# Third layer of a four-layer cross-attention stack: TensorE keeps the written order, dense work spread evenly over the attention units

## The chip, the cores and the metric

One core of a Trainium2 chip runs the whole program in one launch. TensorE (PE) multiplies, VectorE (DVE), ScalarE (ACT) and GpSimd (POOL) do the rest, and every transfer is issued from SyncE's queue (SP). The metric is device time in microseconds; before the change the median of three runs is 1750.37 us (1742.13 to 1756.63).

## The reference, cut to what matters

Four cross-attention layers act one after the other on `x` (8 batches, 256 tokens, 512 features); each takes its keys and values from the same context `ctx` (8, 256, 512).

```python
x = L0(x, ctx)   # layer norm, 16 heads, output projection, then a feed-forward block of width 2048
x = L1(x, ctx)   # one head of width 512:
#   scores = (x Wq^T)(ctx Wk^T)^T / sqrt(512);  x + alpha * softmax(scores) (ctx Wv^T) Wo^T
x = L2(x, ctx)   # 32 query heads of width 16 on 8 key/value heads:
#   q = x Wq + bq;  k = ctx Wk + bk;  v = ctx Wv + bv
#   scores = q k^T / 4 + mask[l, s];  out = softmax(scores) v Wo + bo
#   layer norm of (out + x), times gamma, plus beta
x = L3(x, ctx)   # 16 heads on the layer norm of ctx; x + tanh(gate) * out Wo^T
```

All of it is fp32. The change is about L2, the third layer, and about L1, whose work is done in its shadow.

## The kernel before, in words

**Number format.** Most products use a split of each fp32 operand into a high and a low part (`split`, L175) and three matmuls (`PASSES`: hi-hi, hi-lo, lo-hi). A projection (`feat_mm`, L208, output with features on partitions; `tok_mm`, L222, output with tokens on partitions) is therefore 12 matmuls for one output bank.

**Stages.** First L0's projections and attention, then its feed-forward block (`FeedForward`), whose last of 16 steps is mixed with the beginning of L1 (`mix(ff.steps(1), l12_fill())`). Then one loop, `pipeline` (L717), runs 64 attention *units*: 32 of class `Gqa` (L2: batch b, feature quarter ft) and 32 of class `Mha` (L3).

**A unit of L2.** It has four methods that run in different turns of the loop. In turn t, unit t does A, unit t-1 does B, unit t-2 does C and D.
- A(h), h = 0 to 3 (L1172): two score matmuls (L1179, 512 columns) into the two `sm` banks; DVE adds the mask and takes the maxima with four instructions (L1189). After h = 3, DVE writes the negated maxima as a high and low part.
- B (L1207): PE transposes these (L1210), ACT copies them, SP stores them into rows 96 to 99 of the unit's query stack.
- C(i), i = 0 to 3 (L1225): two matmuls give transposed scores less the maximum (L1233) in the two `st` banks. For the places listed in `POOL_ADDS`, ACT copies the bank out (L1243) and POOL adds the mask (L1244); for the others DVE adds it straight from the bank (L1246). ACT takes the exponential of both halves (L1248).
- The value run `AV(kt)` (L1254) multiplies the probabilities by the values: four matmuls of 32 output rows which use different quarters of the array, a denominator among their rows. AV(0) stands at the end of C(2), AV(1) at the beginning of D.
- D then copies the result out (L1272), stores it to DRAM and loads it in another layout (L1273, L1277); E, later, divides and splits it into `at` (L1285 to L1290).

The unit's query stack comes from `q2d` in DRAM (L1169), its keys from `k2d` (L1170); both loads are issued one turn ahead.

**Dense work.** Everything that isn't attention is written as Python generators kept by `Fillers`. Each `yield` gives a nominal cost in us. After each quarter of a turn the loop calls `fill.tick(us, budget/4)`, which runs generators until the budget of nominal us is spent; in L2 the budget is `B2` = 13 a turn. `fill.until(cond)` runs them regardless of the budget until something that must come first has been written: `before2` (L1442) demands that batch b's queries are written (`ready[0] > b`) one turn ahead of the batch's first unit. The generators of this part:
- `l12_fill` (L1298): for each batch b, L1 and L2's projections. `Context(b).load` fetches weights (`ws`, 1 MB each, three buffers) and the context (`nat`, two buffers, shared with the q stores), `scores_side` multiplies the context by folded weights, `kv` makes L2's keys and values (L1050 stores), `rows` L1's value rows; class `L1` does `features` (transposes), `scores` (softmax on the way), `transpose`, `output`; then `to_feat` and `feat_out` (L354) make L2's queries and store them to `q2d` (L374). Batch b's part starts `LEAD` = 4 turns ahead of its first unit.
- `l2_post` (L1391): the output projection with `wo` and `at`, residual, layer norm, store to `h2d`. It is put at the head of the queue when a batch's last E has been written. It frees the residual's buffer, which a later `L1.load` takes (`free_h`).
- `l3_fill` (L1346): L3's weights and projections; added in `before2` at the last batch of L2.

**What sets the order.** The Python order is only the order in which instructions are written. A list scheduler with a timeline model of the engines then fixes one static order for each engine: among the instructions that are ready in its model it takes the one of highest priority, by order of writing, with A and C raised by `tc.high_priority(PRIO)`. So TensorE may run later units' scores while written-earlier dense work waits. On the chip each engine runs its static order and waits on semaphores.

**Buffers.** PSUM has eight banks: three for dense work and transposes (`pp`), two `sm`, two `st`, one `av`. Probabilities use three `P` buffers and, for batches up to NB - 3, two halves of `pk`.

Of the kernel before, what the change touches and what calls it, by code (L numbers as in the profile page):

```python
# [23 lines left out]
B2, B3 = 13, 5.0  # L24
LEAD = 4
# [43 lines left out]
L3_SB = dict(L_SB, wk="a8-9", wv="a2,a7", x8="a4-5", st5="a3", vo="b3,b4", V="v0-1",  # L69
# [6 lines left out]
def tile_xattn_stack(  # L76
# [131 lines left out]
    def feat_mm(pt, ws, ft, xs, n=D):  # L208
        k = 0
        for kc in range(4):  # L210
            for wj, xj in PASSES:
                nc.tensor.matmul(  # L212
                    pt[:, :n],
                    lhsT=sel(ws, wj, kc)[:, ft * P : (ft + 1) * P],
                    rhs=sel(xs, xj, kc),
                    start=(k == 0),
                    stop=(k == 11),
                )
                k += 1
        return 12 * n * MMUS  # L220

    def tok_mm(pt, xs, tt, ws, n=D):  # L222
        k = 0
        for kc in range(4):
            for xj, wj in PASSES:
# [7 lines left out]
                k += 1  # L233
        return 12 * n * MMUS

# [19 lines left out]

    class Fillers:


        def __init__(self):
            self.q = []  # L260
            self.now = 0.0
            self.acc = 0.0
            self.step = 0

# [14 lines left out]
        def one(self):  # L279
            for e in self.q:  # L280
# [5 lines left out]
        def adv(self, e):  # L286
            try:
# [3 lines left out]
                return  # L291
            if c < 0.0:
# [5 lines left out]
        def until(self, cond):  # L298
            n = 0
            while not cond():  # L300
                self.adv(self.q[0])
                n += 1
                assert n < 9000

# [49 lines left out]
    def feat_out(ph, b, xs, wq, qd, biases):  # L354
        g, bb = divmod(b, 2)
        for f2 in range(2):
            pt = ph.PS("pp")
            for i in range(2):
                c = feat_mm(pt[:, i * 256 : (i + 1) * 256], wq, 2 * f2 + i, xs, n=256)
# [18 lines left out]
            yield 2 * c  # L378
# [338 lines left out]
    def pipeline(units, before, after, budget):  # L717
        n, lag = len(units), 2
        late = []
        for t in range(n + lag + 1):  # L720
            fill.step = t
            if t == 0:
# [9 lines left out]
            for i in range(nch):  # L732
# [6 lines left out]
                if i == nch // 2 - 1 and w:  # L739
                    w.B()  # L740
                fill.tick(us, budget(t) / nch)
                while late and late[0][0] <= fill.now:
# [3 lines left out]
            if v:  # L746
                v.D()
                late.append((fill.now + v.ELAG, t - lag))
# [259 lines left out]
    class Context:  # L1008
# [19 lines left out]
        def scores_side(self):  # L1028
            self.es = kept("ec")[:, 0:1024].rearrange("p (k t) -> p k t", k=4)
            for i in range(2):  # L1030
                pt = ph5.PS("pp")
                for k in range(2):
                    c = feat_mm(pt[:, k * 256 : (k + 1) * 256], self.we, 2 * i + k, self.xs, n=256)
                p3 = pt.rearrange("p (k t) -> p k t", k=2)
                nc.scalar.copy(self.es[:, 2 * i : 2 * i + 2], p3)
                yield 2 * c
            self.wn = load_hl(ph5, mnd, "ws")
# [32 lines left out]
        def rows(self, kt):  # L1070
            self.cp = kept("ec")[:, 1024:].rearrange("p (k n) -> p k n", k=2)
            pt = ph5.PS("pp")
            c = tok_mm(pt, self.xs, kt, self.wn)
            nc.scalar.copy(self.cp[:, kt, :], pt)
            yield c

    class L1:
# [17 lines left out]
        def scores(self, es):  # L1095
            sc = 1.0 / 512.0**0.5
            pt = ph5.PS("pp")
            for qt in range(2):
                for kc in range(4):
# [6 lines left out]
                    )  # L1106
            nb = ph5.T([P, 2], F, "sm1")
# [16 lines left out]
            yield 16 * D * MMUS  # L1124
# [29 lines left out]
    POOL_ADDS = ((0, 1), (1, 1), (2, 1))  # L1154

    class Gqa:
# [59 lines left out]
        def probs(self):  # L1216
            last["p"] = (last.get("p", -1) + 1) % 5
            if self.b < NB - 2 and last["p"] % 2:
# [5 lines left out]
        def C(self, i):  # L1224
            ph = self.ph  # L1225
            kt, hp = divmod(i, 2)
            if i == 0:
                self.av = ph.PS("av")
# [21 lines left out]
            if i == 2:  # L1250
                self.AV(0)


        def AV(self, kt):  # L1254
            with Burst() as mm:
                for hp in (1, 0):
                    for u in range(2):
                        g = 2 * u + hp
                        mm(
                            self.av[32 * g : 32 * g + 32, :],  # L1260
                            self.vo[:, kt, 2 * self.ft + u, :],
                            self.ps[2 * kt + hp][:, u].rearrange("p h t -> p (h t)"),
                            kt == 0,
                            kt == 1,
                        )

        def D(self):
            self.AV(1)
# [28 lines left out]

    def l12_fill():  # L1298
# [4 lines left out]
        yield from c.scores_side()  # L1303
        yield from c.kv()
        for kt in range(2):
            yield from c.rows(kt)
        a.features()
        for b in range(NB):
# [5 lines left out]
            if d:  # L1314
                d.load()
                yield from d.scores_side()
            a.transpose()
            if d:
                nxt = L1(b + 1)
                nxt.load()  # L1320
                while fill.step < 4 * b - 2 and b > 1:
                    yield -1.0
                yield from d.kv()
            yield from a.output(c.cp)
            if b == 0:
                while ff.fc < 4 * NG:
                    yield -0.5
                wts["q2"] = load_w(ph5, w2q, "wq", scale=0.25, stag="nat")
                rows["bo"], rows["g"], rows["b"] = (bcrow(ph5, n) for n in ("bo2", "g2", "b2"))
# [6 lines left out]
            if d:  # L1336
                yield from d.rows(1)
                a = nxt
                a.features()
                yield 2 * TR  # L1340
            yield from feat_out(ph5, b, xs, wts["q2"], q2d, bq25)
            ready[0] += 1
            c = d


    def l3_fill():  # L1346
        free_h.append("a6")
# [18 lines left out]
        while True:  # L1366
            job = None
            if nq < NB and nq in posted and (nq <= nk or nk == NB):
# [22 lines left out]
    def l2_post(b, at):  # L1391
        hb = hts[b]
        for tt in range(2):
            pt = ph5.PS("pp")
            c = tok_mm(pt, at, tt, wts["o2"])
            nc.vector.tensor_tensor(hb[tt], pt, hb[tt], ALU.add)
            yield c
# [24 lines left out]
    fill.add(mix(ff.steps(1), l12_fill()))  # L1422
    fill.until(lambda: ff.n == 4 * NG)
# [18 lines left out]
    def before2(t):  # L1442
# [4 lines left out]
        if b == NB - 1:  # L1447
            fill.add(l3_fill())
# [10 lines left out]
    def before3(t):  # L1459
        b, ft = divmod(t - n2, 4)  # L1460
        if b == 0:
# [12 lines left out]
    def after(t):  # L1474
# [14 lines left out]
        lambda t: B2 if t < n2 else B3,  # L1489
# [102 lines left out]
```

## Time and profile before

| what | value |
|---|---|
| median of 3 runs | 1750.37 us |
| profiled execution, its own time | 1749.14 us |
| its span | 1747.4 us |
| busy: PE, DVE, ACT, POOL | 1616.0, 1085.8, 864.0, 731.1 us |
| mean granted clock of PE | 0.958 |
| first and last score matmul of L2 (L1179) | 839.9 and 1434.4 us |
| last value run of L2 copied out (L1272) | 1470.0 us |
| DMA moved | 329.16 MB, mean 188 GB/s |

How to read it: a group line gives the source line, engine, operation, `out<-in` tile names, sizes and the number of instructions; then the busy time and the mean ns of one; then the engine's idle time just ahead of them and what ended it. A timeline line has start, duration, engine and line; brackets hold the idle time before it and its releaser. `PEld` is the weight load that overlaps matmuls, `SPq` a transfer's issue on SP's queue. The granted clock is the share of full speed that TensorE's throttle let through. Line numbers are those of the kernel before.

### The profile page before, as it was taken

The page shows a single profiled execution, that of the slowest core. Times are in us where ns is not written, and L with a number is a line of the kernel's source. Part 1 is how long each engine was busy: PE and PEld are TensorE (multiplying, and loading weights), DVE is VectorE, ACT ScalarE, POOL GpSimd, SP SyncE. Part 2 cuts the span into 40 slices and gives each one's busy share as a digit, 9 for nine tenths or more (in the row PEclk, how much of TensorE's full clock was granted, in tenths as well). Part 3 has the DMA queues.
Part 4 walks back from the last instruction along what each step waited for, and adds up shares of the span by engine and source line. Part 5 has one row for each costly group of instructions (what it writes and reads, how often), then busy time and mean ns, then how long its engine had stood idle before and what let it go on. Part 6 is the DMA issues. An engine that isn't in the chain of part 4 may idle for free.

```text
span 1747.4 us, 28230 instructions
## 1 busy us (share of the span) xinstructions
PE 1616.0 (92%) x9984; PEld 1224.4 (70%) x9984; DVE 1085.8 (62%) x2412; ACT 864.0 (49%) x1531; POOL 731.1 (42%) x760
## 2 busy tenths in 40 slices
PE   7999999999799999999689899898878989999998
PEld 6877867777577878878456576666646767777765
DVE  6258557777757766622567577666777785655433
ACT  5336545554446566632255456454455545544444
POOL 6345145333455565531234445444436563422111
PEclk9999999999999999999789899898989999999999
DMA  8979775555632434285654575656366756776662
GB/s 294 319 240 285 220 234 190 164 153 164 188 129 88 146 119 145 77 290 218 196 175 151 190 240 174 202 177 189 97 198 180 231 164 217 213 220 210 192 182 76
DMA packets 168444, 329.16 MB, mean 188 GB/s; under 512 B 16336, under 2 KB 84336, under 8 KB 162800
## 3 DMA queue, kind: packets, MB, share of 16 engines
q1 hardware_dynamic: 168304, 327.35, 59.1%
q8 instruction: 80, 1.31, 0.3%
q14 instruction: 60, 0.49, 0.1%
HBM read 230.79 MB, written 96.49 MB: 187 GB/s over the span
## 4 chain that ended last, share of the span: by engine, by line
PE 64%; DMA 15%; DVE 9%; ACT 4%; issue 3%; POOL 3%; SPq 2%; DVEq 0%; ACTq 0%; POOLq 0%
PE pp L212 21%; PE pp L226 21%; PE av L588 8%; PE st L669 3%; PE sm L633 3%; PE st L1233 3%; PE sm L1179 2%; DMA stack<-mT 2%; DMA nat<-in_ctxT_dram 2%; DVE sm L1189 1%; DMA ws<-mnd 1%; PE pp L336 1%; PE pp L1143 1%; DMA stack<-q0d 1%; DMA nd<-avd 1%
## 5 line engine op out<-in xcount | busy, mean ns | idle before, releaser
L640 DVE TENSOR_REDUCE negm<-sm 128x2 f32<-128x512 f32 x256 | 169.8, 682 | 125.4 <-PE sm L633 124.7
L677 ACT ACTIVATE P<-st 128x512 f32<-128x512 f32 x256 | 145.7, 594 | 126.5 <-PE st L669 125.0
L212 PE MATMUL pp<-ys,fw 128*128 128x512 f32 x768 | 190.9, 398 | 6.3 <-ACT fw L178 3.8
L226 PE MATMUL pp<-pw,gs 128*128 128x512 f32 x768 | 193.3, 398 | 3.1 <-ACT gs L948 2.6
L212 PE MATMUL pp<-x,wq 128*128 128x256 f32 x1152 | 169.4, 291 | 6.9 <-ACT wq L181 3.1
L212 PEld LDWEIGHTS pp<-ys,fw 128*128 128x128 f32 x768 | 144.0, 191 | 40.4 <-ACT fw L178 4.0
L212 PEld LDWEIGHTS pp<-x,wq 128*128 128x128 f32 x1152 | 156.2, 196 | 20.5 <-issue 6.6
L226 PEld LDWEIGHTS pp<-pw,gs 128*128 128x128 f32 x768 | 142.1, 190 | 38.5 <-ACT gs L948 4.2
L588 PE MATMUL av<-P,V 128*32 128x256 f32 (+1 forms) x2188 | 164.5, 402 | 4.0 <-DVE xt L702 2.9
L1189 DVE CUSTOM_DVE_ANT_0 sm<-sm,va 128x256 f32<-128x256 f32 x256 | 104.8, 440 | 56.2 <-PE sm L1179 55.1
L1179 PE MATMUL sm<-ks,stack 96*128 96x512 f32 x256 | 111.4, 467 | 29.2 <-DMA stack<-q2d 16.3
L949 POOL TENSOR_TENSOR gs<-xt,gs 128x512 fp32r<-128x512 f32 x64 | 91.8, 1442 | 90.8 <-ACT gs L948 90.8
L1189 DVE CUSTOM_DVE_ANT_0 sm<-sm,vb 128x256 f32<-128x256 f32 x256 | 104.4, 440 | 37.8 <-PE sm L1179 36.5
L1233 PE MATMUL st<-stack,ks 100*128 100x512 f32 x256 | 103.7, 459 | 18.2 <-DMA stack<-mT 10.0
L1248 ACT ACTIVATE P<-P 128x1024 f32<-128x1024 f32 x90 | 95.1, 1059 | 50.3 <-POOL P L1244 26.0
L226 PE MATMUL pp<-wo,at 128*128 128x512 f32 x384 | 106.5, 404 | 1.3 <-ACT at L705 1.3
L944 DVE SCALAR_TENSOR_TENSOR xt<-xt,xt 128x512 f32<-128x512 f32 x64 | 66.6, 1045 | 64.5 <-ACT xt L943 64.5
L588 PEld LDWEIGHTS av<-P,V 128*32 128x32 f32 x2188 | 59.0, 109 | 57.6 <-issue 15.4
L179 POOL TENSOR_TENSOR fw<-stg,fw 128x1024 fp32r<-128x1024 f32 x32 | 81.8, 2564 | 34.7 <-ACT fw L178 19.6
L1179 PEld LDWEIGHTS sm<-ks,stack 96*128 96x128 f32 x256 | 51.5, 207 | 63.4 <-issue 30.0
L645 POOL CAST mhl<-negm 128x8 fp32r<-128x8 f32 x64 | 15.9, 249 | 187.7 <-DVE negm L640 187.7
L226 PEld LDWEIGHTS pp<-wo,at 128*128 128x128 f32 x384 | 69.8, 191 | 22.7 <-issue 3.3
(214 smaller groups left out, 3557.0 us busy)
## 6 DMA issues: line engine op xcount, KB each, us to landing
stg<-in_wfc_dram SPq DMA_DIRECT2D x32, 512.0 KB
stg<-in_wpr_dram SPq DMA_DIRECT2D x32, 512.0 KB
ws<-med SPq DMA_DIRECT2D x16, 1024.0 KB
ws<-mnd SPq DMA_DIRECT2D x16, 1024.0 KB
q2d<-nat SPq DMA_DIRECT2D x48, 256.0 KB
stack<-q2d SPq DMA_DIRECT2D x32, 384.0 KB
k0d<-nat SPq DMA_DIRECT2D x16, 512.0 KB
stack<-k0d SPq DMA_DIRECT2D x32, 256.0 KB
```

The source lines that it names most:

```text
L179: lo.tensor_tensor(w[:, 1], stg, fp(w[:, 0]), ALU.subtract)
L212: nc.tensor.matmul(pt[:, :n], lhsT=sel(ws, wj, kc)[:, ft * P : (ft + 1) * P], rhs=sel(xs, xj, kc), start=(k == 0), stop=(k == 11),)
L226: nc.tensor.matmul(pt[:, :n], lhsT=sel(xs, xj, kc)[:, tt * P : (tt + 1) * P], rhs=sel(ws, wj, kc), start=(k == 0), stop=(k == 11),)
L588: self.prev = nc.tensor.matmul(o, lhsT=lhsT, rhs=rhs, start=start, stop=stop, skip_group_check=True).ins
L640: nc.vector.tensor_reduce(self.negm[:, 2 * h : 2 * h + 2], pt.rearrange("p (q k) -> p q k", q=2), AX.X, ALU.max, negate=True)
L677: nc.scalar.activation(p, pt, AF.Exp)
L944: nc.vector.scalar_tensor_tensor(v, v, 1.0 / GA, u, ALU.add, ALU.mult)
L949: nc.gpsimd.tensor_tensor(lo, u, fp(hi), ALU.subtract)
L1179: nc.tensor.matmul(pts[qt], lhsT=self.qs[0:96, h, qt * P : (qt + 1) * P], rhs=self.ks[0:96].rearrange("p u k -> p (u k)"), start=True, sto ...
L1189: nc.vector.tensor_tensor_reduce(out=t, in0=t, in1=self.am[:, qt, :], scale=1.0, scalar=-3.0e38, op0=ALU.add, op1=ALU.max, accum_out=self. ...
L1233: nc.tensor.matmul(pt, lhsT=self.ks[0:100, u, kt * P : (kt + 1) * P], rhs=self.qs[0:100, 2 * hp : 2 * hp + 2, :].rearrange("p h t -> p (h ...
L1248: last["act"] = nc.scalar.activation(pf, pf, AF.Exp).ins
```

## The change

Constants and buffers: `B2` 13 to 8, with 14 for the first three turns; `B3` (L3's budget) 5.0 to 5.5; `LEAD` 4 to 5; L3's value weights move from buffer a7 to a6, so `pk` stays in use for all batches of L2, and the spare residual buffer for L3 is a7 from L3's second batch on (it was a6 from the beginning of `l3_fill`).

Order on TensorE: in turns 1 to 31, each TensorE instruction gets a dependency without a semaphore on the one written before it, so the scheduler must keep the written order; the other engines are scheduled as before.

Dense work in smaller pieces: projections of L1 and L2 yield after half of their matmuls (`Open`), and a generator that has yielded `Open` is continued before any other. `until` sets the balance of the budget to zero from the start of this stage.

L1's steps: batch 0's are all written during the last feed-forward step, batch 1's context work ahead of the first unit; from batch 1 on, the steps of a batch and of the next context are interleaved anew, and `kv` moves from the middle to just ahead of `feat_out`. `l3_fill` starts when `l12_fill` ends.

In the unit: one value run of eight matmuls, kt = 1 first, written in D; in the ordered turns D is written after the first quarter of the next turn. B is written after the second quarter's dense work instead of before it. `POOL_ADDS` gets a fourth place, (3, 1).

```diff
-B2, B3 = 13, 5.0
-LEAD = 4
+B2, B3 = 8.0, 5.5
+LEAD = 5
...
+    def halves(gen, us):
+        for k, _ in enumerate(gen):
+            if k == 5:
+                yield Open(us)
...
         def one(self):
+            if self.open:
+                self.adv(self.open)
+                return True
...
+            self.open = e if isinstance(c, Open) else None
...
+            if self.even:
+                self.acc = 0.0
...
-    def pipeline(units, before, after, budget):
+    def pipeline(units, before, after, budget, ordered=lambda t: False):
...
+        def keep_order(first):
+            for x in nc.cur_bb.bb.instructions[first:]:
+                if x.engine == mybir.EngineType.PE:
+                    if prev[0] is not None:
+                        tc.add_manual_dep(
+                            x,
+                            prev[0].name,
+                            mybir.DependencyInfo(mybir.DependencyClass.NoSync, mybir.DependencyReason.DATA),
+                            reason="keep_order",
+                        )
+                    prev[0] = x
+
+        def finish(e):
+            units[e].D()
+            late.append((fill.now + units[e].ELAG, e))
...
-                if i == nch // 2 - 1 and w:
+                while held:
+                    finish(held.pop())
+                if i == nch // 2 - 1 and w and not ordered(t):
                     w.B()
                 fill.tick(us, budget(t) / nch)
+                if i == nch // 2 - 1 and w and ordered(t):
+                    w.B()
...
             if v:
-                v.D()
-                late.append((fill.now + v.ELAG, t - lag))
+                if ordered(t):
+                    held.append(t - lag)
+                else:
+                    finish(t - lag)
+            if ordered(t):
+                keep_order(first)
+            else:
+                prev[0] = None
...
-    POOL_ADDS = ((0, 1), (1, 1), (2, 1))
+    POOL_ADDS = ((0, 1), (1, 1), (2, 1), (3, 1))
...
-            if self.b < NB - 2 and last["p"] % 2:
+            if last["p"] % 2:
...
-            if i == 2:
-                self.AV(0)
...
-        def AV(self, kt):
+        def AV(self):
             with Burst() as mm:
+                for kt in (1, 0):
+                    for hp in (1, 0):
...
         def D(self):
-            self.AV(1)
+            self.av = self.ph.PS("av")
+            self.AV()
...
+        for b in range(1, NB):
             while fill.step < 4 * b - LEAD:
                 yield -1.0
...
             yield from a.scores(c.es)
             if d:
                 d.load()
-                yield from d.scores_side()
+                yield from d.scores_side(0)
             a.transpose()
+            yield 2 * TR
             if d:
                 nxt = L1(b + 1)
                 nxt.load()
-                while fill.step < 4 * b - 2 and b > 1:
-                    yield -1.0
-                yield from d.kv()
+                yield from d.scores_side(1)
             yield from a.output(c.cp)
...
             if d:
-                yield from d.rows(1)
                 a = nxt
                 a.features()
                 yield 2 * TR
+                yield from d.rows(1)
+                while fill.step < 4 * b - 2 and b > 1:
+                    yield -1.0
+                yield from d.kv()
             yield from feat_out(ph5, b, xs, wts["q2"], q2d, bq25)
             ready[0] += 1
             c = d
+        fill.add(l3_fill())
...
-        lambda t: B2 if t < n2 else B3,
+        lambda t: (14.0 if t < 3 else B2) if t < n2 else B3,
+        lambda t: 0 < t < n2,
```

## Prediction

> **What bounds the kernel now.** I read the page first: TensorE (PE) is busy for 92% of the span, and the slices show where it isn't. The weak stretch is slices 19 to 33, the third layer, which also is the only long stretch with a lowered clock.
>
> ```profile
> span 1747.4 us, 28230 instructions
> ...
> PE   7999999999799999999689899898878989999998
> ...
> DVE  6258557777757766622567577666777785655433
> ...
> PEclk9999999999999999999789899898989999999999
> ```
>
> The windows view gives that stretch, from the first score matmul to the last (840 to 1468), beside a calm stretch of the last layer:
>
> ```profile
> 840.00:1468.00 628.00, 563.70 (x3066) 399.97 (x3067) 449.84 (x1488) 315.10 (x527) 294.36 (x304) 0.92 0.57 180
> ...
> 1476.00:1700.00 224.00, 220.88 (x1875) 170.10 (x1874) 112.42 (x192) 107.31 (x236) 53.82 (x105) 1.00 0.68 207
> ```
>
> Columns are the stretch's length, then busy time of PE, its weight loads, DVE, ACT and POOL, then PE's granted clock. PE idles for 64.3 us of the 628, and 0.08 of the clock is missing. DVE is busy for 72%, so it isn't the bound on average, only locally. The groups of PE by shape in 840 to 1468 say where:
>
> ```profile
> L1179 PE MATMUL sm<-ks,stack 96*128 96x512 f32 x256 | 111.4, 467 | 29.2 <-DMA stack<-q2d 16.3 <-DVE mx L1189 11.3 <-DVE sm L1122 1.1
> L1233 PE MATMUL st<-stack,ks 100*128 100x512 f32 x256 | 103.7, 459 | 18.2 <-DMA stack<-mT 10.0 <-ACT P L1243 4.9 <-DVE P L1246 1.5
> ...
> L226 PE MATMUL pp<-wo,at 128*128 128x512 f32 x168 | 47.6, 405 | 0.0
> ```
>
> A score matmul takes 0.42 us of PE on average, a projection of the same 512 columns 0.28. Scores that come alone are paced by DVE (four maxima of 0.38 us each per pair) and fall into the half clock. In the built order of the instructions, 15 of the 112 score pairs of units 3 to 30 have no dense work before the next pair; after the change 6 have none.
>
> **What the matmuls of the stretch cost.** Rates from starts in the PE timeline: 36 matmuls of 256 columns in 4.63 us (0.129); 12 of 512 in 2.91 (0.24); 24 of 128 in 3.19 (0.13); L1 scores 16 in 3.62; L1 output 0.47 an instruction; a value run of eight 1.06. The changed order has in its stretch 512 scores and 408 projections of 512 columns (221 us), 1037 of 256 columns (134), 144+200+32 of 128 (49), 31 value runs (33), L1 scores and outputs (25+26): 488 us. Before is 491 by the same list. So 628 = 491 + 64 idle + 73 of low clock and switching between streams. The missing clock is at most 0.08 x 628 = 50 us; part of it falls into idle time, and I take 37, which leaves 36 us, 7%, for switching.
>
> **The change, part by part.**
> *Even dense work* (budget 13 to 8, halves, lead 5, L1's steps spread): it removes no matmul. It takes the score-only stretches away, so their idle time and half clock go: stretch = 488 x 1.07 = 524 us before any new wait.
>
> *TensorE in written order*: waits that the scheduler filled with other units' scores are now PE's own. Two recur.
> First, the next context. Its load into `nat` follows the q2d stores on SP's queue, and `scores_side` needs it. A batch boundary of before:
>
> ```profile
> 1180.37 2.88 PE L212 MATMUL pp<-x,wq 128*128 128x256 f32 x23
> ...
> 1183.56 3.62 PE L1100 MATMUL pp<-ec,x 128*128 128x256 f32 x16
> ...
> 1192.13 0.40 PE L1179 MATMUL sm<-ks,stack 96*128 96x512 f32 x1
> 1196.08 0.79 PE L212 MATMUL pp<-x,ws 128*128 128x256 f32 x2 [3.56 <-ACT x L178]
> ```
> ```profile
> 1188.62 0.92 SPq L1017 DMA_DIRECT2D nat<-in_ctxT_dram  x1
> ```
> ```profile
> 1195.41 1.14 ACT L178 CAST x<-nat 128x512 fp32r<-128x512 f32 x2 [3.68 <-DMA nat<-in_ctxT_dram]
> ```
>
> From the last q matmul (about 1183.6; one more follows the line shown) to the first use it took 12.5 us, in the boundary before (1107.5 to 1121.57) 14.1. In the written order only L1's scores (3.6), one step of scores (4 x 0.24) and one value run (1.06) lie between, 5.6 us; behind the wait stand all scores, so DVE and ACT run dry too. Also `kv` now comes just ahead of feat_out, so the 1 MB weights in its buffer load in the same stretch. Ends: 1.8 us (7.1/4, what PE pays now at this place) and 8.5 (14.1 - 5.6); I take 5, nearer the strict end. The clock after such a gap:
>
> ```profile
> 1192.00:1196.00 4.00, 0.53 (x2) 0.08 (x1) 2.91 (x12) 0.59 (x2) 2.46 (x3) 0.83 0.93 315
> 1196.00:1200.00 4.00, 3.92 (x14) 3.34 (x14) 2.62 (x9) 4.00 (x9) 3.89 (x4) 0.50 0.36 99
> 1200.00:1204.00 4.00, 4.00 (x26) 2.31 (x25) 1.30 (x7) 1.59 (x2) 1.68 (x3) 0.82 1.01 278
> ```
>
> That is 4 x 0.5 + 4 x 0.18 = 2.7 us of clock; I add 2.5. Six contexts: 6 x 7.5 = 45 us. The Trainium skill (TensorE: Matmul & The Clock Gate, "HAM oscillation — how this bites in real kernels") speaks against the change here: idle gaps over about 3.4 us bring the half clock back; the row agrees, and the page's window at half rate would make it 1.7 us a gap, 5 us less in all. A second page differs from the rows: DMA: Bandwidth & Descriptors ("Anatomy of one DMA — SWDGE (gpsimd) path") gives 2 us plus the bytes at 436 GB/s, an estimate of 3.2 us for the 512 KB that took 6.8 here; by it the wait would be 1.4 us, under the gate's window, and the total some 36 us lower. The row decides.
>
> Second, the one value run. It now waits for the last probabilities, whose second mask add moves from DVE to POOL. The chain of such a piece:
>
> ```profile
> 1101.62 0.40 PE L1233 MATMUL st<-stack,ks 100*128 100x512 f32 x1
> ...
> 1102.05 0.59 ACT L1243 COPY P<-st 128x512 f32<-128x512 f32 x1 [0.37 <-PE st L1233]
> ...
> 1102.71 1.28 POOL L1244 TENSOR_TENSOR P<-P,vb 128x512 f32<-128x512 f32 x1 [2.13 <-ACT P L1243]
> ...
> 1104.14 1.06 ACT L1248 ACTIVATE P<-P 128x1024 f32<-128x1024 f32 x1 [0.55 <-DVE sm L318]
> ```
>
> It ends 3.6 us after its matmul began. PE has 0.48 + the step's dense work + 0.96 to do; the built order's last steps hold 3072, 1024, 3072 and 7168 columns in a batch's four units (1.55, 1.04, 1.55, over 3 us), which leaves 0.6, 1.1, 0.6 and 0: 0.6 on average. ACT waits 1.0 us each (26.0/26) for POOL now, so ends 0 and 2; I take 0.9, x 31 = 28 us.
>
> The rest: L2's output projection follows E by one step and may wait for `at`, and L1's next rows come 1.5 units after the store that frees their buffer; together 1 us a batch, 6 us (ends 0 and 30: before's chain from the add at 1099.5 to a load issued at 1117.0 is 17.5 us, about one unit). The maxima's transpose moves behind one step's dense work; two steps still cover its DMA, and its 17 us of waits now are part of the idle time removed. POOL's extra add (1.28 x 32 = 41 us; 294 of 628 busy) and ACT's copy (0.59 x 32; 315 of 628) hide beside PE; DVE loses 0.69 x 32. Keeping `pk` for all units and one less spare h buffer cost nothing while PE has dense work queued. Stretch: 524 + 45 + 28 + 6 = 603, so 25 less than 628.
>
> *The start*: PE waits 10.06 us at 839.92 for the first q2d. Now context 1's scores_side, kv and transposes are written between (6.2 + 4.8 + 1 us): -10 (ends -10 and 0).
>
> *Outside*: the last layer gets 67 matmuls of 256 and 12 of 512 columns more (+14 at its slower rates), the work ahead of the stretch about 9 us less: +5. Its budget of 5.5 for 5.0 changes nothing while PE is full there.
>
> **Sum.** The profiled execution took 1749.14 us, 1.2 below the median of 1750.37. 1749 - 25 - 10 + 5 = **1719 us**.
>
> **Rivals.**
> *The new waits stay hidden*: context 1.8 us without cold clock, values 0: 524 + 11 + 6 = 541; 1749 - 87 - 10 + 5 = **1657**. For: one batch's load could go earlier. Against: q2d's stores stand ahead of it on SP.
> *The waits only move*: context 8.5 + 2.5, values 1.5: 524 + 66 + 46 + 6 = 642; **1758**. For: the 14.1 us row. Against: DVE and ACT are emptier at that place.
> *Slower, by the value run*: if POOL's fourth add queues behind the third and behind E's multiplies, every unit pays 3.0 us: 524 + 45 + 93 + 6 = 668; **1784**. It turns slower from about 2.5 us a run on. For: it is behind an engine given 41 us more; against: ACT's wait for POOL never exceeded 2.3 us.
>
> **How the numbers follow.** Forecast 0.37 (1690 to 1748), hidden 0.25, moved 0.18, slower 0.20. A difference of 1%, 17 us, is about what can be told from no change. Below 1732: 0.25 + 0.32 = 0.57; within 1%: 0.05 + 0.16 = 0.21; above 1767: 0.20 + 0.02 = 0.22. The range 1650 to 1780 cuts about half of each outer case.
>
> **What would show it.** Right: the stretch near 603 us, scores at 0.28 us each, clock near 1.00 but for a dip at each context, waits of PE on the context's split near 30 us and on the last exponentials near 28. Wrong: no PE wait on the context (then 1657), PE waiting on DVE's maxima as now (then evenness did nothing), or value-run waits over 75 us.

## The result, and the profile after

The changed kernel takes 1820.83 us (median, 1816.96 to 1825.94), the kernel before, in the same rounds, 1746.39 (1742.13 to 1756.63): ratio 1.0406, 95% interval 1.0374 to 1.0437. It is 4% slower; 1719 had been forecast, and the range ended at 1780. The profiled execution took 1816.96 us, its span is 1815.0.

The page of after: the same lines as of before.

```profile
span 1815.0 us, 28390 instructions
...
PE   7999989999899999997877888888957688999998
...
DVE  6267457777667676433555656657756573654443
...
PEclk9999989999999999998988989899969899999999
```

The weak stretch is weaker: PE's slices 19 to 33 now hold mostly 7 and 8, down to 5, where 8 and 9 stood, and DVE's fell too. So no other engine became the bound; everything waits more. The windows view, from the start of the first score matmul to that of the last (used so from here on), first of before, then of after:

```profile
839.92:1464.31 624.39, 560.09 (x3047) 396.93 (x3048) 447.82 (x1485) 312.50 (x522) 291.26 (x300) 0.92 0.57 181
1464.31:1747.00 282.69, 271.24 (x2318) 202.90 (x2316) 135.60 (x232) 136.85 (x302) 67.72 (x132) 1.00 0.62 189
```
```profile
822.56:1511.73 689.17, 556.71 (x2999) 401.63 (x3000) 420.48 (x1448) 328.67 (x554) 325.49 (x325) 0.90 0.51 167
```

By place, the 67.6 us between the spans are: ahead of the stretch -17.4 (839.92 to 822.56), the stretch +64.8, behind it +20.2 (283.1 to 303.3). In the stretch PE's busy time hardly moved (560 to 557), its idle time doubled: 64.3 to 132.5 us. The waits of PE in the stretch of after (total, times, longest):

```profile
PE pp L212 <- ACT x L178: 25.5, 5, 6.8
PE av L620 <- ACT P L1312: 16.4, 10, 5.1
PE pp L367 <- DVE h L354: 15.1, 1, 15.1
PE sm L1244 <- DVE mx L1254: 12.9, 18, 1.4
PE av L620 <- ACT pk L1312: 12.6, 6, 5.1
PE st L1297 <- DMA stack<-mT: 10.6, 4, 5.8
PE pp L212 <- ACT wq L181: 9.3, 1, 9.3
...
PE pp L212 <- POOL x L179: 4.1, 5, 1.0
```

In order: the next context's split (25.5 + 4.1), the last exponentials of the one value run (16.4 + 12.6), a wait for rows of a context in the last layer's preparation, the maxima on DVE, the transposed maxima's DMA, the last layer's weights. The groups of the scores by shape, where 467 and 459 ns stood:

```profile
L1244 PE MATMUL sm<-ks,stack 96*128 96x512 f32 x256 | 103.5, 470 | 21.1 <-DVE mx L1254 12.9 <-PE pp L226 3.0 <-issue 1.2
L1297 PE MATMUL st<-stack,ks 100*128 100x512 f32 x256 | 86.7, 418 | 10.8 <-DMA stack<-mT 10.6 <-ACT P L1307 0.2
```

A score still costs 0.37 us of PE on average ((103.5 + 86.7) / 512; 0.42 before), not 0.28.

### The profile page after: what moved, and what is told of

It is laid out like the page before. It is cut to its first block, busy times and chain, and to the rows that moved or that the text cites. A ratio compares the mean times of both kernels' runs of the same rounds, so it can differ in the third digit from the quotient of the medians.

```text
span 1815.0 us, 28390 instructions
## 1 busy us (share of the span) xinstructions
PE 1618.7 (89%) x9984; PEld 1234.2 (68%) x9984; DVE 1068.4 (59%) x2380; ACT 883.2 (49%) x1563; POOL 773.4 (43%) x792
## 4 chain that ended last, share of the span: by engine, by line
PE 29%; DMA 8%; DVE 6%; POOL 2%; ACT 2%; issue 2%; SPq 1%; DVEq 0%; ACTq 0%; POOLq 0%
PE pp L226 8%; PE pp L212 7%; PE av L620 6%; PE sm L1244 2%; DMA stack<-mT 2%; DVE sm L1254 2%; PE st L1297 2%; PE sm L665 2%; PE st L701 2%; DMA q2d<-nat 1%; DMA nat<-in_ctxT_dram 1%; DMA h2d<-h 1%; DMA avd<-xt 1%; DMA nd<-avd 1%; PE pp L367 1%
## 5 line engine op out<-in xcount | busy, mean ns | idle before, releaser
L212 PE MATMUL pp<-x,wq 128*128 128x256 f32 x1152 | 161.8, 292 | 12.0 <-ACT wq L181 9.6
L212 PEld LDWEIGHTS pp<-x,wq 128*128 128x128 f32 x1152 | 151.9, 197 | 24.3 <-ACT wq L181 10.1
L1244 PE MATMUL sm<-ks,stack 96*128 96x512 f32 x256 | 103.5, 470 | 21.1 <-DVE mx L1254 12.9
L1312 ACT ACTIVATE P<-P 128x1024 f32<-128x1024 f32 x77 | 81.5, 1059 | 53.8 <-POOL P L1308 42.1
L212 PE MATMUL pp<-x,ws 128*128 128x256 f32 x480 | 74.8, 312 | 30.0 <-ACT x L178 25.5
L212 PEld LDWEIGHTS pp<-x,ws 128*128 128x128 f32 x480 | 70.5, 216 | 38.9 <-ACT x L178 27.5
L1297 PE MATMUL st<-stack,ks 100*128 100x512 f32 x256 | 86.7, 418 | 10.8 <-DMA stack<-mT 10.6
```

Source lines behind the costliest of these rows:

```text
L212: nc.tensor.matmul(pt[:, :n], lhsT=sel(ws, wj, kc)[:, ft * P : (ft + 1) * P], rhs=sel(xs, xj, kc), start=(k == 0), stop=(k == 11),)
L1244: nc.tensor.matmul(pts[qt], lhsT=self.qs[0:96, h, qt * P : (qt + 1) * P], rhs=self.ks[0:96].rearrange("p u k -> p (u k)"), start=True, sto ...
L1297: nc.tensor.matmul(pt, lhsT=self.ks[0:100, u, kt * P : (kt + 1) * P], rhs=self.qs[0:100, 2 * hp : 2 * hp + 2, :].rearrange("p h t -> p (h ...
L1312: last["act"] = nc.scalar.activation(pf, pf, AF.Exp).ins
```

## The experiments

Two theories stood at first. One: the written order lays open waits that the scheduler had filled. The rival: the other parts (later `kv`, one value run, a fourth add on POOL, one buffer less, other budgets) cost the time. Times are medians; "before" is the median of the same call, 1746.6 to 1751.7. A ratio compares with the kernel before in the same rounds; its 95% interval is some 0.3 to 0.5% wide to each side, 5 to 9 us, so a difference of 4 to 7 us between two kernels isn't clear of noise.

The table has the windows of the profiled executions that the text compares ("behind" is the rest of the span). Its last two columns are a count in the PE timeline: of the 128 pairs of score matmuls (A), those after which PE does no dense work and none of the last layer's before the next pair, here called score-only, and PE's idle time from such a pair to the next one.

| kernel | ahead | stretch | PE busy | PE idle | clock | behind | score-only pairs | idle in them |
|---|---|---|---|---|---|---|---|---|
| before | 839.9 | 624.4 | 560.1 | 64.3 | 0.92 | 283.1 | 18 | 16 |
| after | 822.6 | 689.2 | 556.7 | 132.5 | 0.90 | 303.3 | 8 | 8 |
| a_free | 825.8 | 630.9 | 561.7 | 69.2 | 0.92 | 309.0 | 16 | 14 |
| b_order | 840.8 | 761.3 | 630.6 | 130.7 | 0.81 | 291.2 | 76 | 98 |
| c_all | 824.8 | 625.9 | 542.2 | 83.7 | 0.93 | 305.2 | 3 | 2.5 |
| f_all | 827.3 | 631.4 | 557.8 | 73.5 | 0.92 | 305.4 | 10 | 14 |
| f_coarse | 827.8 | 666.3 | 593.0 | 73.3 | 0.93 | 271.4 | 16 | 20 |
| b_even | 846.9 | 647.6 | 564.9 | 82.7 | 0.88 | 362.4 | 35 | 31 |
| f_l12 | 831.7 | 613.3 | 552.4 | 60.8 | 0.92 | 309.3 | 20 | 24 |

### The order alone, and all but the order

*a_free*: after, without the dependencies.

```diff
-            if ordered(t):
-                keep_order(first)
-            else:
-                prev[0] = None
+            prev[0] = None
```

> The changed kernel without the written order on TensorE: the scheduler may again put other units' matmuls into a wait; every other part stays (even budgets, halves, one value run, four GpSimd adds, buffers). Theory (the written order exposes the waits, 131 us of TensorE waits in the stretch against 64 before): the exposed waits on the context's split, the last exponentials and the stores fall from some 60 us to under 25, and the time is 1730 to 1760. Rival (the other parts cost it: later kv, one value run, four adds, one spare buffer less): 1800 or more, with the order worth under 20 us.

Measured 1766.37; ratio to before 1.0104 [1.005, 1.0159]. The order costs 54 us of the 74 (1821 to 1766, and 1746 to 1821). The context's waits fall to 6.7 us and those on the exponentials to 1.5, but other waits stand in the list:

```profile
PE st L1294 <- DMA stack<-mT: 17.9, 10, 3.8
PE sm L1241 <- DVE mx L1251: 14.8, 24, 2.9
PE pp L1150 <- DMA h<-h1d: 6.4, 3, 3.4
PE pp L226 <- DMA ws<-mnd: 6.3, 6, 3.5
PE pp L212 <- ACT x L178: 6.0, 4, 2.3
```

The time is 6 us above what the theory expected, and 16 to 20 us stay with the other parts. Both theories hold a share; the order has the larger.

*b_order*: before, with `keep_order` as in the change, over the same steps.

```diff
         lambda t: B2 if t < n2 else B3,
+        lambda t: 0 < t < n2,
```

> The kernel before with nothing but the written order on TensorE added, over the same steps of the third layer. Theory (the order alone costs): over 1800, since bursts of scores, two value runs a unit and the coarse dense pieces stand in a fixed order too. Rival (the order is harmless, the other parts cost): within 20 us of 1746.

Measured 1895.88; 1.0825 [1.077, 1.0879]. The mean clock in its stretch is 0.81. The waits of PE there:

```profile
PE av L588 <- ACT P L1267: 46.9, 27, 3.2
PE sm L1198 <- DVE mx L1208: 37.1, 52, 3.4
PE av L588 <- ACT pk L1267: 27.1, 14, 2.9
```

With two value runs a unit, they wait 41 times for exponentials (74 us), and the scores wait 52 times for the maxima. In the fixed order of the old parts 76 of the 128 score pairs are score-only (18 before), and these hold 98 of the 131 us of idle time. So under the written order the change's other parts are worth 75 us (1896 to 1821); under the scheduler's they cost 16 (1750 to 1766): they pay only together with the order.

### The waits under the written order, one at a time

*a_pool3*: the fourth add back to DVE.

```diff
-    POOL_ADDS = ((0, 1), (1, 1), (2, 1), (3, 1))
+    POOL_ADDS = ((0, 1), (1, 1), (2, 1))
```

> The changed kernel with GpSimd's fourth mask add given back to VectorE (three places as before). If the fourth add delays the last exponentials that the value run waits for (29 us of TensorE waits now): 10 to 25 us less than 1821. If that wait comes from the one value run's place and not from GpSimd: within 6 us of 1821.

Measured 1808.71, 12 less. The value run's waits go from 29.0 to 3.3 us:

```profile
PE pp L212 <- ACT x L178: 24.2, 5, 5.7
PE sm L1244 <- DVE mx L1254: 17.8, 24, 1.5
PE pp L367 <- DVE h L354: 16.0, 1, 16.0
PE sm L1244 <- issue: 9.2, 7, 1.6
...
PE av L620 <- ACT P L1312: 3.3, 3, 2.2
```

So it was the POOL add, as the expectation had it; of 26 us of waits that go, 12 come off the time. Waits on DVE's maxima and at issue grew by 13.

*a_l3free*: the order only up to step 23.

```diff
-            if ordered(t):
+            if ordered(t) and t < 24:
                 keep_order(first)
```

> The changed kernel with the written order only up to step 23; the last eight steps of the stretch, in which the last layer's preparation runs beside the scores, are left to the scheduler. If the spare buffer's late release and the late weights under the written order (waits of 15.1 and 9.3 us, clock 0.67) make half of the loss: 1780 to 1795. If the loss is spread over all batches: over 1805.

Measured 1811.01, 10 less: the loss is not one of the end, it is spread.

*c_ctx*: q written ahead of `kv` in the loop.

```diff
+            yield from feat_out(ph5, b, xs, wts["q2"], q2d, bq25)
+            ready[0] += 1
+            if d:
                 while fill.step < 4 * b - 2 and b > 1:
                     yield -1.0
                 yield from d.kv()
-            yield from feat_out(ph5, b, xs, wts["q2"], q2d, bq25)
-            ready[0] += 1
```

> The changed kernel, written order and all, with the q projection of a batch written ahead of the next context's k and v instead of behind it, so that 4.7 us of dense work stand between the q stores and the first use of the next context's load. If the context waits (29.6 us of TensorE waits in the stretch) are a cost of this order of writing: 12 to 30 us less than 1821, waits on the context's split under 12 us. If they only move (to the weights or to the values that kv makes): within 6 us of 1821.

Measured 1814.27, 6.5 less (ratio 1.0365 [1.0326, 1.0404], so not clear of noise). The context's waits halve (29.6 to 13.4), but 17.4 + 9.9 on the exponentials stay, and 9.6 on the split of transposed rows is new: between the two expectations, nearer to "they only move".

*c_spare*: a buffer lent once to the last layer's preparation. The gap that it is aimed at, in after: SP, DVE, then PE, and the clock in windows of 4 us.

```profile
1404.11 0.43 SPq L1492 DMA_DIRECT2D h2d<-h  x1
...
1405.23 0.52 SPq L1492 DMA_DIRECT2D h2d<-h  x1
1411.18 0.38 SPq L446 DMA_DIRECT2D h<-in_ctxn_dram  x1
```
```profile
1414.89 1.29 DVE L348 BATCH_NORM_STATS2 st<-h 128x6 f32<-128x512 f32 x2 [10.09 <-DMA h<-in_ctxn_dram]
```
```profile
1402.01 1.04 PE L367 MATMUL pp<-ident,h 128*128 128x128 f32 x8
1418.15 2.21 PE L367 MATMUL pp<-ident,h 128*128 128x128 f32 x8 [15.10 <-DVE h L354]
```
```profile
1402.00:1406.00 4.00, 1.05 (x9) 0.80 (x7) 2.80 (x9) 2.41 (x5) 4.00 (x4) 1.00 0.50 165
1406.00:1410.00 4.00, 0.00 (x0) 0.00 (x0) 0.00 (x0) 0.51 (x1) 1.22 (x3) 0.65 0.45 157
...
1418.00:1422.00 4.00, 3.85 (x13) 3.22 (x14) 2.50 (x9) 0.77 (x2) 0.54 (x1) 0.50 0.15 9
1422.00:1426.00 4.00, 4.00 (x22) 3.75 (x21) 4.00 (x14) 2.30 (x4) 2.08 (x3) 0.71 0.34 126
```

The load of a context's rows goes into the buffer out of which batch rows are still stored; it is issued 6 us after the second store, DVE gets the rows at 1414.9, and all of PE stands behind the transposes of these rows, scores included, as DVE, ACT and POOL then do.

```diff
     def l3_fill():
+        free_h.append("a3")
...
-            free_h.append(self.slot)
+            if self.slot != "a3":
+                free_h.append(self.slot)
```

> The changed kernel with one buffer more for rows at the start of the last layer's preparation (a3, which is free there), lent once. The 15.1 us wait at 1403, in which a load waits for stores out of the only buffer, should go. Theory (it is a cost of the buffer taken away together with the written order): 12 to 20 us less than 1821. Rival (the work behind it is short of other data anyway): under 6 us less.

Measured 1817.08, 4 less, which is within the noise (1.0382 [1.0348, 1.0416]). The wait goes, and in its place 8.1 us of waits stand at the same transposes for other rows (`h2d`). The rival fits: one gap of 15 us was worth some 4, as the data of the next job was late too.

*c_bearly*: the transpose of the maxima ahead of the step's dense work, as before.

```diff
-                if i == nch // 2 - 1 and w and not ordered(t):
+                if i == nch // 2 - 1 and w:
                     w.B()
                 fill.tick(us, budget(t) / nch)
-                if i == nch // 2 - 1 and w and ordered(t):
-                    w.B()
```

> The changed kernel with one line moved back: the maxima's transpose ahead of the step's dense work, as before the change; written order and four GpSimd adds stay. If the transpose's place only costs its own waits (10.6 us on the stack's load): 1806 to 1818. If the four mends helped together mostly by this one (they made 53 us where the value run's, the context's and the buffer's mends alone made 12, 6 and 4): under 1795.

Measured 1814.27, 6.5 less (1.0369 [1.0319, 1.0419], not clear of noise); waits on `stack<-mT` go from 10.6 to 2.2.

### The mends together

*c_poolb* has the edits of a_pool3 and c_bearly, *c_cs* those of c_ctx and c_spare, *c_all* all four, *f_all* all four without the order.

> The changed kernel with three GpSimd adds and the transpose moved back, written order kept. If waits of two units in flight add up (transpose early and exponentials early, both feed the step after): 1770 to 1790. If the effects of the two are separate: the sum of what each makes alone, 12 us and that of the transpose.

Measured 1799.36: 21 less, 18.5 being the sum of the two. Within the noise they add up.

> The changed kernel, written order and four GpSimd adds kept, with two mends together: q ahead of kv, and the lent buffer. Alone these made 6.5 and 4 us; with the two other mends (together 21) all four made 53. If the two stand on one chain (a wait that goes in one place comes back at the other): 1785 to 1798, over 20 us below 1821. If the surplus of 53 over the parts comes from the joint work of all four: 1805 or more.

Measured 1803.15: 18 less by the medians, where 10.5 is the sum. But the kernel before was faster in these rounds: by the ratio (1.0347 [1.03, 1.0393], after's is 1.0406) it is 10 less, just the sum. So no gain beyond the sum is shown. The median lies between the two expectations.

> The changed kernel, written order kept, with four mends together: q ahead of kv, the lent buffer, GpSimd's fourth add given back, the maxima's transpose ahead of the step's dense work. If the named waits are all that the written order costs, their sum goes (about 22 context, 15 buffer, 12 value run, 6 maxima): 1755 to 1775. If each wait that goes only lays open the next: 1785 or more.

Measured 1767.55; 1.0111 [1.0065, 1.0157]. The four are worth 53 us, the two pairs 39; by the ratios it is 52 and 30. Part of this surplus of 14 to 21 may be the spread (c_all's four runs lie between 1757.67 and 1772.45, and the profile is of the shortest); the rest isn't explained. PE's waits in its stretch:

```profile
PE sm L1243 <- issue: 13.1, 7, 3.1
PE sm L1243 <- DVE mx L1253: 10.5, 20, 1.7
PE pp L212 <- ACT x L178: 9.3, 2, 4.9
PE pp L367 <- DVE h L354: 8.5, 1, 8.5
PE pp L367 <- DVE nat L396: 8.4, 2, 8.1
...
PE av L621 <- ACT P L1311: 4.4, 2, 3.5
...
PE st L1296 <- DMA stack<-mT: 0.9, 1, 0.9
```

At the four places after had 84 us of waits (29.6, 29.0, 15.1 and 10.6); some 25 are left, so 59 went and the time fell by 53. The single mends took away 26, 16, 15 and 8 us of waits for 12, 6.5, 4 and 6.5. That one mend brings the next wait to light fits the lists of a_pool3 and c_spare; that it explains the whole difference isn't shown.

> The same four mends without the written order. If the order costs more than the named waits: 1735 to 1755, 15 or more below the same with the order. If the mends do what the scheduler did: equal to it within 8 us.

Measured 1765.81; 1.0096 [1.0063, 1.0129]. With the four mends no cost of the order shows any more (1768 with, 1766 without), and without the order no gain of the mends (a_free 1766, f_all 1766). Mending by hand gives about what the scheduler gives without it. c_all has 3 score-only pairs and f_all 10, at the same time.

### What the even budgets are worth

*b_even*: before, with the numbers of the change alone (budget 8, in the first three steps 14; 5.5; lead 5).

```diff
-B2, B3 = 13, 5.0
-LEAD = 4
+B2, B3 = 8.0, 5.5
+LEAD = 5
...
-        lambda t: B2 if t < n2 else B3,
+        lambda t: (14.0 if t < 3 else B2) if t < n2 else B3,
```

> The kernel before with the numbers of the changed one and nothing else: budget 8 for 13 (14 in the first three steps), 5.5 for 5.0, lead 5 for 4; no halves, no order, two value runs, three adds. If even dense work is worth what was forecast for it (no score-only stretches, so less idle time and no half clock): 1690 to 1735. If the scheduler makes the work even by itself and the numbers only carry work into the last layer: 1745 to 1775.

Measured 1854.75; 1.0592 [1.0534, 1.065]: far outside both. Stretch, then the rest:

```profile
846.91:1494.51 647.60, 564.89 (x2786) 371.13 (x2787) 436.33 (x1454) 300.00 (x501) 279.69 (x287) 0.88 0.50 160
1494.51:1856.00 361.49, 331.49 (x2582) 252.01 (x2578) 150.33 (x262) 149.60 (x323) 76.46 (x144) 0.93 0.55 172
```

The stretch holds 261 matmuls fewer than before's (2786 for 3047) and is 23 us longer all the same; the work comes back in the last layer, which takes 79 us more. So the stretch isn't shortened by taking dense work out of it: what it lacks, PE then lacks as filling. And b_even isn't even: with the smaller budget in the old loop 35 score pairs are score-only, where before had 18, and they hold 31 of its 83 us of idle time. It shows what too small a budget costs there, not what evenness is worth.

*f_coarse*: f_all with the budgets of before.

```diff
-B2, B3 = 8.0, 5.5
+B2, B3 = 13, 5.0
```

> The changed kernel without written order and with the four mends, and with the budgets of before (13 and 5.0; lead 5). If the even budgets cost the last 18 us: 1740 to 1755. If they are harmless and the value run, the halves or the buffers cost it: 1760 to 1775.

Measured 1767.53 (the 14 of the first three turns stays in it). In the profile 329 matmuls move from behind into the stretch (2958 to 3287), which grows by 35 us while the rest shrinks by 34. Here budgets only carry work to and fro. With the larger budget 16 pairs are score-only, 10 in f_all; the idle time is the same (73.3 and 73.5 us).

### The rest of 18 us

*f_av2*: f_all with two value runs a unit, the second at the step's end.

```diff
             if i == 0:
+                self.av = ph.PS("av")
                 self.ps = []
...
             self.ps.append(p)
+            if i == 2:
+                self.AV(0)
...
         def D(self):
-            self.av = self.ph.PS("av")
-            self.AV()
+            self.AV(1)
...
-                if ordered(t):
-                    held.append(t - lag)
-                else:
-                    finish(t - lag)
+                finish(t - lag)
```
(`AV` multiplies one `kt` at a time again.)

> The four mends without the written order, and with the value runs of before: two a unit, the second at the step's end. f_all took 1766, before 1748. If the one late value run costs the rest: 1742 to 1755. If not: 1760 to 1775, and the rest lies in the order in which the dense work is written or in its halves.

Measured 1763.80; 1.0119 [1.0072, 1.0167]. Not the value run.

*f_l12*: f_all with the loop over the batches of before.

```diff
-                yield from d.scores_side(0)
+                for i in range(2):
+                    yield from d.scores_side(i)
             a.transpose()
-            yield 2 * TR
...
-                yield from d.scores_side(1)
+                while fill.step < 4 * b - 2 and b > 1:
+                    yield -1.0
+                yield from d.kv()
             yield from a.output(c.cp)
```
(`rows(1)` goes ahead of `features()` again, and `kv` is gone from the end.)

> f_all (four mends, no written order, 1766) with the loop over the batches written as before the change: both halves of the scores' side together, kv right behind, then output, rows, q. If the new order of the dense work costs the rest: 1742 to 1755. If not: 1760 to 1775.

Measured 1742.68; 0.997 [0.9944, 0.9996]. In the kernel with halves, the spread of L1's steps and the late `kv` make 23 us; this is the only version that beats before, by 0.3%. It isn't the more even one: 20 of its pairs are score-only, 10 in f_all.

```profile
831.67:1444.94 613.27, 552.44 (x3029) 399.58 (x3027) 440.77 (x1482) 313.42 (x526) 287.88 (x294) 0.92 0.56 187
```

Against f_all the stretch holds 71 matmuls more (2958 there) and is 18 us shorter, though this profile is of the kernel's slowest run (1756).

*f_whole*: f_all with whole pieces, an `Open` step being joined to the one behind it in `adv`. *f_l12w*: f_l12 with the same.

```diff
                 c = next(e[0])
+                while isinstance(c, Open):
+                    c = float(c) + next(e[0])
...
-            self.open = e if isinstance(c, Open) else None
```

> f_all with whole pieces of dense work instead of halves, all else the same. If the smaller pieces cost the rest (more changes between streams on TensorE): 1742 to 1755. If pieces of half the size make TensorE fuller, as the forecast had it: 1775 or more. If neither: within 6 us of 1766.

> f_l12 (1743, before 1747) with whole pieces of dense work instead of halves. In f_all whole pieces made 9 us less. If that adds to the order of the loop: 1728 to 1738, 0.5 to 1% below before, what is left of the change being the opening, one value run and even budgets. If not: 1740 to 1750.

Measured 1756.42 (1.0055 [1.0029, 1.0081]) and 1752.76 (1.0025 [0.9996, 1.0054]). Whole pieces help by 9 in the changed loop and cost 10 in the old one; a rule can't be read from that, and the gains don't add. With whole pieces the old loop is worth 4 us (1756 to 1753), with halves 23: the loss belongs to the two together, not to the loop alone.

*b_start*: before, with the changed opening alone.

```diff
...
-        for b in range(NB):
+        c = Context(1)
+        c.load()
+        a = L1(1)
+        a.load()
+        yield from feat_out(ph5, 0, xs, wts["q2"], q2d, bq25)
+        ready[0] += 1
+        yield from c.scores_side()
+        yield from c.kv()
...
+        for b in range(1, NB):
```

> The kernel before with the changed opening of the third layer alone: the first q projection is written ahead of context 1's multiplications, so these lie beside the first q stores; later batches, budgets and everything else stay. By the term for the start in the forecast, -10 (ends -10 and 0), and the 9 us of work that leaves the time ahead and comes back beside it: 1736 to 1745. If the ten us come back in the stretch: 1746 to 1755.

Measured 1750.68 against 1746.58; 1.0024 [0.9995, 1.0053]. The first score comes at 820.24 for 839.92, and the kernel isn't shorter: in the profiled execution, its shortest (1735), the stretch is 8 us longer, and the median gives back all of it.

## Why the prediction was wrong

*The step that failed* is the first part: "It takes the score-only stretches away, so their idle time and half clock go: stretch = 488 x 1.07 = 524 us before any new wait." That is 104 us less than 628 for the other parts of the change: all 64 us of idle time, the 37 of clock, and 3 of less work. This put all idle time and most of the missing clock down to score-only stretches, and no row split them. Counted from one score pair to the next in before's trace, score-only pairs hold 16 of the 64 us of idle time and 12 of the 51 us of missing clock. So some 28 us stand in them, where 101 were taken; low clock that lasts into the steps behind them isn't in this count. The other 48 us of idle time stand beside dense work. The largest waits of the whole stretch were for the queries' load (16.3 us), the maxima (11.3), the transposed maxima (10.0) and the next context (7.1).

Measured without the order (a_free), the other parts leave 16 score-only pairs of 18, the stretch at 630.9 for 624.4, idle time at 69.2 for 64.3, the clock at 0.92: a gain of 104 was forecast and +6.5 came. With the order such pairs do become few, 8 in after and 3 in c_all, and what they cost goes (8 us of idle time and 1 of clock in after). But beside dense work the idle time grows from 48 us to 125 in after and 81 in c_all. So a step with dense work in it idles too, and more even work didn't remove those waits. The order was over-priced, if anything: 79 us were added for it, and from a_free to after the stretch grows by 58.

*Switching at 7%* was wrong as well. Two units of before, with PE full:

```profile
1000.00:1040.00 40.00, 40.00 (x240) 30.41 (x240) 28.73 (x105) 20.87 (x34) 15.89 (x18) 1.00 0.69 222
```

In it lie 35 scores, 48 projections of 512 columns, 79 of 256, 24 of 128, 32 value matmuls, 4 L1 outputs, 18 transposes; at the prices of the prediction (transposes 8 in 1.04) 8.4 + 11.5 + 10.2 + 3.1 + 4.2 + 1.9 + 2.3 = 41.6 us, in 40.0. No cost of changing between streams shows here. By the prediction's list PE's busy time is 69 us too long in both kernels (560 for 491, 557 for 488). The missing clock, weighted by PE's busy time in windows of 4 us, is 39 us of that in before and 43 in after; the other 30 and 26 aren't explained (b_order has 29 of the kind). So the 68 us that PE idles longer in after cost next to no clock in its busy time. In b_order, whose idle time is as long as after's but in 115 waits of 1.2 us on average (82 of 1.6 in after), the same sum gives 110 us and PE's busy time grows by 70: there idle time was paid twice. It is the kernel with 76 score-only pairs, and 113 of the 148 us of clock that its stretch misses stand in them.

*The context*: a wait of 30 us forecast (6 x 5), 29.6 measured. *The value run*: 28 forecast, 29.0 measured, and the POOL add was its cause. Both were right in size, and as both were sums of guesses between wide ends, some luck is in it. But neither is a price: taken away, 16 and 26 us of waits gave 6.5 and 12. Adding waits up as if each came off the time is a wrong step of the sum, hidden here by a far larger one. The second page that the prediction sets against its rows is, as its heading says, about transfers issued by GpSimd; the load of the context is issued on SP's queue, so its 6.8 us don't speak against that page.

*"One less spare h buffer cost nothing while PE has dense work queued"* failed: work queued behind the waiting transpose can't be used in a written order. One wait of 15.1 us; mended alone, some 4.

*"Two steps still cover its DMA"*, of the maxima's transpose, failed: 10.6 us of waits stay, where before had 10.0, and moved back it gives some 6.5. The "17 us of waits now" were misread: 7.0 of them are waits of weight loads, not of PE's matmuls.

*The start and the work ahead*: -19 forecast, -17.4 measured, in the trace; b_start shows that alone it is no gain. *The last layer*: +14 forecast, +20.2 measured.

*The rivals*: the slower one had the right sign by the wrong mechanism: 3.0 us a value run, where 29.0 / 31 = 0.9 was paid. None had "evenness does nothing" with a price, though the prediction named it as what would prove it wrong; and that sign came: PE waits 11.3 us on DVE's maxima before and 12.9 after.

*The skill's rule against the change* was that of the Trainium skill (TensorE: Matmul & The Clock Gate, "HAM oscillation — how this bites in real kernels"): gaps over some 3.4 us bring the half clock back. The rows of the 15.1 us gap agree in kind: PE went idle at 1403.05; a mean of 0.65 in 1406 to 1410 puts the fall at about 1407.2, 4.1 us later; 0.71 in 1422 to 1426 puts the return at about 1424.3, 6.2 us after work began at 1418.15. But such a gap isn't needed. In before, gaps of about 1 us between pairs of scores were enough:

```profile
1115.64 1.10 PE L1179 MATMUL sm<-ks,stack 96*128 96x512 f32 x2 [1.06 <-DVE sm L1122]
1117.79 1.19 PE L1179 MATMUL sm<-ks,stack 96*128 96x512 f32 x2 [1.06 <-DVE mx L1189]
```
```profile
1114.00:1116.00 2.00, 0.94 (x3) 0.37 (x2) 1.74 (x10) 0.74 (x4) 0.00 (x0) 1.00 1.14 383
1116.00:1118.00 2.00, 0.94 (x3) 0.45 (x2) 1.72 (x8) 0.00 (x0) 0.00 (x0) 0.53 0.81 232
1118.00:1120.00 2.00, 0.99 (x3) 0.37 (x3) 1.43 (x8) 0.00 (x0) 0.00 (x0) 0.50 1.06 360
```

PE is busy for half of this time, and the clock falls at about 1116.1. b_order, with the lowest clock of all, has one wait over 3.4 us in its stretch (10.2, the first). So the length of a single gap alone doesn't decide it in this case; where page and rows differ, the rows decide. The prediction's price for the gate, 2.5 us for each of six gaps, wasn't checked gap by gap; the whole stretch of after lost only 4 us more of clock in PE's busy time than that of before.

## What to carry to other kernels

Before a gain from "even" work is counted, split the idle time in the trace by what stands there: here a quarter of it (16 of 64 us) stood where dense work was missing, and a count in the order of instructions doesn't show that. A fixed order on an engine turns every late input into a wait of all that stands behind it, so price all waits that the scheduler had filled, not only the recurring ones; or run the order alone first (here 145 us on the old parts, 54 on the new). A wait isn't a price: alone, four mends took 8 to 26 us of waits away for 4 to 12 us of time, together 59 for 53.

## What the runs showed that was not expected

The same budgets are harmless in the changed kernel without the order (f_coarse against f_all, 2 us) and, with a lead of 5 for 4, cost 103 us in the kernel before (b_even). And 23 us hang on the sequence in which the same projections of a batch are written, with no order kept at all (f_all 1766, f_l12 1743), but only 4 when the pieces are whole (f_whole, f_l12w). Which wait carries this isn't settled: in f_all `stack<-mT` makes 19.2 us of waits and in f_l12 9.5, but the two profiles differ in more than that. Nor was the written order tried with f_l12's loop.
